# A post-norm stack of eight layers on one core: the last sequence's output map and norms in two halves of 128 tokens

## The chip, the core and the metric

The kernel runs on one core of one Trainium2 chip. A core has five engines that run side by side and wait for one another by semaphores: PE (matrix products and transposes), DVE (elementwise and reductions), ACT (functions and copies), POOL (elementwise) and SP (which issues most DMAs). The metric is the device time of one execution in microseconds; times are medians of several runs.

## The reference, cut to what matters

Eight layers in a row, each with a residual and a norm over the 128 features. Only the last two matter here: an attention over 8 sequences of 256 tokens with 16 heads of 8 features, and a linear map with ternary weights. The reference works them out like this (the four kinds of heads, rotation and decay, are left out):

```python
out = jnp.einsum('bhqk,bhkd->bhqd', attn, v)
out = jnp.transpose(out, (0, 2, 1, 3)).reshape(b, n, H * dh)
return out @ w_o
...
w_eff = w_ternary * alpha
out = jnp.einsum('bsd,od->bso', input, w_eff) + bias
...
x = _layernorm(x + _L3_attn_ref(x, ...), axis=-1)
x = _layernorm(x + _L3_ffn_ref(x, ...), axis=-1)
```

So after the attention every token goes, by itself, through the output map, a norm, the ternary map and a second norm. The attention is causal: the first 128 tokens of a sequence look at 128 keys, the last 128 at 256.

## The kernel before, in words

The program has six stages; the change is in the last, `typed` (from L2301), which computes the two layers above. Its work comes in 48 units, six for each of the 8 sequences. A unit is written (t, r0, r1): t = 0 takes the first 128 tokens, t = 1 the last 128, and r0 to r1 picks heads. So a sequence has the units (0, 0, 4), (0, 4, 8), (1, 0, 2), (1, 2, 4), (1, 4, 6), (1, 6, 8): two for the first half of its tokens and four for the second. The text names them by the first two numbers.

Each unit goes through the same steps, spread over four rounds of the loop over `i`: scores on PE (`sc`, with the decay and the mask added by small matmuls), row maxima on DVE (`nm`, L2254), Exp on ACT (`e`, L2259), the division by the sums on POOL (`e`, L2262), eight transposes on PE (`pt`, L981), two copies to SBUF on DVE or ACT (`ptsb`, L983), and 16 small matmuls into the output tile (`o`, called at L2271). The tile `o` holds one sequence, features by 256 tokens, in the one PSUM bank with the tag O: units with t = 0 fill its columns 0 to 127, the others columns 128 to 255.

After the sixth unit of a sequence comes its tail, the generator `after` (L2305): ACT copies `o` to SBUF (`ot`, L2308); PE multiplies by the output map (`wo`, four matmuls for the two token tiles); DVE adds the residual (L2316); `token_norm` (L942) takes statistics on DVE (L948, L949), Ln and Exp on ACT (L951, L952) and scales on DVE (L955); `channels` (L957) transposes the two tiles on PE (`zt`, L961) and copies them on ACT (`s_t`, L962), while POOL adds the bias rows (L2321); PE multiplies by the ternary map (`lin`); DVE adds (L2328); a second norm, a second pair of transposes and a last copy (`s3`) follow, and SP writes 128 x 256 values to the output (L2334).

Four results of a tail pass through PSUM: `wo`, `zt`, `lin` and `zt` again. All of them take the tag M, which has a single bank in this stage (`BANKS`: A=2, B=2, O=1, M=1). So do the projections of the next sequences.

A tail is not written in one piece. Its steps are put, as a generator, into the queue `side`, and the loop takes up to three steps per round from the head of that queue; a generator is finished before the next in the queue begins.

The order in which this writes instructions down is not the order in which the engines get them. At the end of the build the class `_Order` plans the whole program: it follows a model of the engines with a table of lengths, and at each moment gives a free engine the ready instruction with the lowest rank. A rank is the instruction's place in the program plus an offset from the table `BIAS`, by engine, tile name and stage (for instance 4960 for `DVE nm` in this stage, and 1645 for `DVE st`). The offsets and lengths were set for the program as it was; the change leaves them as they are. Two of the planner's rules matter here:

```python
if self.rings[tag][next_[tag]] != k:
    return None
...
if t.space == PSUM and self.ops[j][1] != e:
    self.edge(j, i)
```

The first: the tiles of one tag get their buffers strictly in program order. The second: two engines that use the same PSUM tile keep their program order, whichever columns they use.

Of the kernel before, what the change touches and what calls it, by code (L numbers as in the profile page):

```python
# [14 lines left out]
F32 = mybir.dt.float32  # L15
BF = mybir.dt.bfloat16
I32 = mybir.dt.int32
AF = mybir.ActivationFunctionType
ALU = mybir.AluOpType
# [4 lines left out]
P = 128  # L24
B = 8
S = 256
# [745 lines left out]
class _Kernel:  # L772
# [169 lines left out]
    def token_norm(self, src, dst, small, eps=EPS):  # L942

        nc = self.nc
        st = small.tile([P, 2, 6], F32, tag="st", name="st")
        mv = small.tile([P, 2, 2], F32, tag="mv", name="mv")
        for t in range(2):
            nc.vector.bn_stats(st[:, t, :], src[:, t, :])  # L948
            nc.vector.bn_aggr(mv[:, t, :], st[:, t, :])  # L949
        rs = small.tile([P, 2], F32, tag="rs", name="rs")  # L950
        nc.scalar.activation(rs, mv[:, :, 1], AF.Ln, bias=eps)  # L951
        self.norm = nc.scalar.activation(rs, rs, AF.Exp, scale=-0.5)  # L952
        yield
        for t in range(2):
            nc.vector.tensor_scalar(dst[:, t, :], src[:, t, :], mv[:, t, 0:1], rs[:, t : t + 1], ALU.subtract, ALU.mult)  # L955

    def channels(self, z, dst, copy, tag="M"):  # L957

        ps = self.psum(tag, "zt")
        for t in range(2):  # L960
            self.nc.tensor.transpose(ps[:, t * P : (t + 1) * P], z[:, t, :], self.ident)  # L961
        copy(dst, ps[:, 0:S])  # L962

    def softmax(self, small, work, sc, groups, keys, tag):

# [1335 lines left out]
    def typed(self):  # L2301
        nc, work, small = self.nc, self.ty, self.tys
        we, decay, inputs, before = self.we, self.decay, self.inputs, self.typed_before

        def after(b, o):  # L2305
            cs = bass.ts(b, S)
            ot = work.tile([P, S], F32, tag="ot", name="ot")
            nc.scalar.copy(ot, o)  # L2308
            yield
            ps = self.psum("M", "wo")[:, 0:S]  # L2310
            for t in range(2):
                ts = slice(t * P, (t + 1) * P)
                self.mm(ps[:, ts], ot[:, ts], self.w3[:, 640:768], t == 0, t == 1)
            s = work.tile([P, 2, P], F32, tag="s", name="s")
            flat = lambda a: a.rearrange("p t d -> p (t d)")
            nc.vector.tensor_add(flat(s), ps, flat(self.rows(b)))  # L2316
            yield from self.token_norm(s, s, small)
            yield
            st = work.tile([P, S], F32, tag="st", name="s_t")
            self.channels(s, st, nc.scalar.copy)  # L2320
            nc.gpsimd.tensor_tensor(s, s, self.bias3.unsqueeze(1).to_broadcast([P, 2, P]), ALU.add)  # L2321
            yield
            ps = self.psum("M", "lin")[:, 0:S]
            for t in range(2):
                ts = slice(t * P, (t + 1) * P)
                self.mm(ps[:, ts], st[:, ts], we, t == 0, t == 1)
            s2 = work.tile([P, 2, P], F32, tag="s2", name="s2")
            nc.vector.tensor_add(flat(s2), ps, flat(s))  # L2328
            yield from self.token_norm(s2, s2, small)
            yield  # L2330
            s3 = work.tile([P, S], F32, tag="s3", name="s3")
            self.channels(s2, s3, nc.scalar.copy)
            yield
            nc.sync.dma_start(self.out[:, cs], s3)  # L2334

        units = [(b, u) for b in range(B) for u in [(0, 0, 4), (0, 4, 8)] + [(1, r, r + 2) for r in range(0, 8, 2)]]
        n = len(units)
        side = deque([chain(self.results(1, work), before(1))])
        scs, es, o = {}, {}, None

        for i in range(n + 3):
            last = pts = None
            if i >= 3:
                pts = self.typed_transposed(es.pop(i - 3), work)
                last = self.last
            if i < n:
                b, u = units[i]
                while b not in inputs:  # L2350
                    if next(side[0], True):
                        side.popleft()
                scs[i], last = self.typed_scores(u, *inputs[b][:2], decay, last)
            if 0 <= i - 1 < n:
                es[i - 1] = self.typed_softmax(units[i - 1][1], scs.pop(i - 1), work, small)
            for _ in range(2):
                if side and next(side[0], True):
                    side.popleft()
            if i >= 3:
                b, u = units[i - 3]  # L2360
                if u[:2] == (0, 0):
                    o = self.psum("O", "o")[:, 0:S]
                    if b + 2 < B:
                        side.append(self.results(b + 2, work))
                self.typed_outputs(u, pts, inputs[b][2], o, last)
                if u[:2] == (1, 6):
                    rest = after(b, o)
                    next(rest)
                    if b + 2 < B:
                        side.append(before(b + 2))  # L2370
                    side.append(rest)
            if side and next(side[0], True):
                side.popleft()
        for g in side:
            for _ in g:
                pass
# [34 lines left out]
```

## Time and profile before

| what | value |
|---|---|
| median of three runs | 1642.47 us (1641.91 to 1643.14) |
| the profiled execution's own time | 1644.68 us |
| its span, first to last instruction | 1642.9 us |
| PE busy in the span | 1417.4 us (86%) |
| DVE, ACT, POOL busy | 1102.3, 968.6, 587.5 us |
| last sixteen matmuls of `o` end | 1629.43 us |
| last copy ends, output DMA is issued | 1638.31, 1638.34 us |
| mean granted clock of PE | 0.942 |

Positions are microseconds from the start of the span. In the timeline a line shows the start, the time taken, the engine, the line of the kernel, the operation and its tiles with their sizes; "x16" joins sixteen instructions in a row, and brackets tell how long the engine had been idle and what ended that. In the chain of waits a line is a piece of the chain that ended last: start, time, engine, tile and line; "issue" is a moment in which the engine waited for nothing that the profile shows. In the table by stretches a line gives from:to, length, then the busy time and number of instructions of PE, PE's weight loads, DVE, ACT and POOL, then the granted clock, the DMA share and GB/s.

### The profile page before, as it was taken

Reading aid. Unit: us, or ns where it says so; the run is one execution under the profiler, and the core shown is the slowest. Engines: PE = TensorE matmul, PEld = TensorE weight load, DVE = VectorE, ACT = ScalarE, POOL = GpSimd, SP = SyncE. Lnnn points to the kernel's source line nnn. Section 1 sums busy time; section 2 is a strip of 40 time slices with the busy share of each in tenths; the row PEclk is TensorE's granted clock in tenths of the full one; section 3 lists DMA queues with packets and bytes.
Section 4 is the critical chain, followed back from the end, with each engine's and each line's share of the span. In section 5 each row is a group of like instructions: output and inputs, shape, how many; then the busy total and the mean of one; then the engine's idle time right before and its main releaser. Section 6 shows DMA issues by size and latency. Waiting matters only on the chain. (4 is left out here: it accounts for less than half of the span.)

```text
span 1642.9 us, 28581 instructions
## 1 busy us (share of the span) xinstructions
PE 1417.4 (86%) x10826; PEld 909.4 (55%) x10826; DVE 1102.3 (67%) x2182; ACT 968.6 (59%) x2656; POOL 587.5 (36%) x535
## 2 busy tenths in 40 slices
PE   2688998989898887777579999999998899899997
PEld 1354554545554544334366766777675576556664
DVE  5745568898989898698545557554546333279886
ACT  3777888787978869446125545455453222167775
POOL 1334544535462523101431222212212102467774
PEclk7789999989999999779789999999998899999998
DMA  5000012121212223155430000000000130000000
GB/s 199 1 1 1 1 40 65 40 60 45 65 40 65 53 52 91 52 179 189 151 119 1 8 12 11 10 5 8 32 18 24 46 121 26 26 9 8 5 8 11
DMA packets 45113, 77.97 MB, mean 47 GB/s; under 512 B 5580, under 2 KB 21988, under 8 KB 43824
## 3 DMA queue, kind: packets, MB, share of 16 engines
q1 hardware_dynamic: 39648, 70.02, 14.0%
q0 software_dynamic: 3216, 5.07, 1.1%
q8 instruction: 85, 1.39, 0.4%
q10 hardware_dynamic: 2112, 1.05, 0.2%
q14 instruction: 52, 0.43, 0.1%
HBM read 66.87 MB, written 10.76 MB: 47 GB/s over the span
## 5 line engine op out<-in xcount | busy, mean ns | idle before, releaser
L870 PE MATMUL y<-hs,ident 128*128 128x512 f32 x256 | 139.7, 659 | 35.9 <-DVE hs L1307 35.6
L1158 POOL TENSOR_TENSOR e<-e,rc 128x1024 f32<-128x1024 f32 x32 | 78.0, 2437 | 202.7 <-DVE rc L1157 194.3
L1306 DVE TENSOR_TENSOR_SCAN hs<-da,hs 128x1024 f32<-128x1024 f32 x64 | 149.1, 2331 | 0.2
L2259 ACT ACTIVATE e<-sc,nm 128x128 f32<-128x128 f32 (+1 forms) x256 | 105.2, 427 | 46.6 <-DVE nm L2254 40.3
L1153 ACT ACTIVATE e<-sc,nm,rn 128x128 f32<-128x128 f32 x256 | 114.3, 466 | 13.8 <-DVE nm L1148 13.5
L981 PE MATMUL pt<-ident,e 128*128 128x128 f32 x768 | 114.2, 278 | 9.4 <-POOL e L1158 4.9
L1302 ACT ACTIVATE da<-d,na 128x255 f32<-128x255 f32 x256 | 109.3, 504 | 17.5 <-DVE hs L1306 13.7
L1836 POOL TENSOR_TENSOR e<-e,rc 128x512 f32<-128x512 f32 x32 | 34.0, 1064 | 219.8 <-DVE rc L1835 154.2
L981 PEld LDWEIGHTS pt<-ident,e 128*128 128x128 f32 x768 | 88.5, 141 | 42.5 <-issue 16.1
L2262 POOL TENSOR_TENSOR e<-e,rc 128x1024 f32<-128x1024 f32 x48 | 90.8, 1896 | 39.1 <-DVE rc L2261 32.1
L1105 POOL TENSOR_TENSOR t<-t,t 128x512 f32<-128x512 f32 x64 | 83.9, 1316 | 58.0 <-DVE t L1092 51.6
L1811 ACT COPY kp<-kps 128x512 f32<-128x512 f32 x128 | 74.7, 583 | 49.0 <-PE kps L870 46.4
L1658 POOL DMA_INDIRECT got<-ybuf,get x48 | 45.7, 952 | 159.2 <-DMA ybuf<-ys 97.1
L870 PEld LDWEIGHTS y<-hs,ident 128*128 128x128 f32 x256 | 48.5, 205 | 82.5 <-DVE hs L1307 54.2
L1304 DVE TENSOR_TENSOR hs<-u,bc 128x1024 f32<-128x1024 f32 x64 | 84.3, 1328 | 2.9 <-POOL u L1291 2.9
L1307 DVE TENSOR_TENSOR hs<-hs,bc 128x1024 f32<-128x1024 f32 x64 | 80.6, 1260 | 0.0
L1847 ACT COPY vs<-vps 128x512 f32<-128x512 f32 x64 | 37.4, 585 | 67.1 <-PE vps L870 53.6
L983 DVE COPY ptsb<-pt 128x512 f32<-128x512 f32 x104 | 68.8, 675 | 11.6 <-PE pt L981 9.3
L870 PE MATMUL qk<-w_local,h 128*128 128x512 f32 x128 | 69.3, 631 | 7.5 <-DVE t L1092 7.1
L870 PE MATMUL vps<-sa_vp,x_lf 128*32 128x512 f32 x512 | 68.4, 594 | 0.0
L1847 DVE COPY vs<-vps 128x512 f32<-128x512 f32 x64 | 43.3, 682 | 37.2 <-PE vps L870 25.1
L2057 DVE TENSOR_TENSOR sh<-sh,pu 128x512 f32<-128x512 f32 x32 | 22.0, 688 | 67.1 <-PE pu L870 54.0
(380 smaller groups left out, 3782.4 us busy)
## 6 DMA issues: line engine op xcount, KB each, us to landing
bc<-xs SPq DMA_DIRECT2D x128, 256.0 KB
w_moe<-in_e_dram SPq DMA_DIRECT2D x16, 768.0 KB
w_attn<-in_w_dram SPq DMA_DIRECT2D x4, 1024.0 KB
w_local<-in_w_dram SPq DMA_DIRECT2D x2, 1557.0 KB
places<-zeros SPq DMA_DIRECT2D x2, 1280.0 KB
got<-places SPq DMA_DIRECT2D x6, 256.0 KB
ybuf<-ys SPq DMA_DIRECT2D x8, 160.0 KB
x_in<-in_x_dram SPq DMA_DIRECT2D x1, 1024.0 KB
```

Source lines behind the costliest of these rows:

```text
L870: return self.nc.tensor.matmul(out, lhsT, rhs, start=start, stop=stop)
L981: self.last = self.nc.tensor.transpose(pt[:, j * P : (j + 1) * P], src[:, j * P : (j + 1) * P], self.ident)
L1105: nc.gpsimd.tensor_add(t1, t1, t2)
L1153: nc.scalar.activation(e[:, j, g, :], scs[:, j, g, :], AF.Exp, bias=nm[:, j, g : g + 1], scale=rq[:, j, g : g + 1], accum_out=sm[:, j, g : ...
L1158: nc.gpsimd.tensor_tensor(e, e, rc.unsqueeze(3).to_broadcast([P, 2, 4, P]), ALU.mult)
L1302: nc.scalar.activation(da[:, n, c, 1:S], d[:, c, 1:S], AF.Exp, scale=na[:, i : i + 1])
L1304: nc.vector.tensor_tensor(hs, u.unsqueeze(1).to_broadcast(shp), bn, ALU.mult)
L1306: nc.vector.tensor_tensor_scan(line(hs), line(da), line(hs), 0.0, ALU.mult, ALU.add)
L1307: nc.vector.tensor_tensor(hs, hs, cn, ALU.mult)
L1847: i = copy(v[:, c, :, :].rearrange("p a b -> p (a b)"), ps)
L2259: nc.scalar.activation(e[:, i, :], sc[:, i, :], AF.Exp, bias=nm[:, i : i + 1], accum_out=sm[:, i : i + 1])
L2262: nc.gpsimd.tensor_tensor(e, e, rc.unsqueeze(2).to_broadcast([P, n, keys]), ALU.mult)
```

## The change

For the last sequence (b = 7) the tail is run twice, each time for 128 tokens. The first half starts after the unit (0, 4), when columns 0 to 127 of `o` are complete: `after(b, o, (0,))` is begun there (its `ot` copy), and its other steps go to the end of the queue `side`. The second half starts after (1, 6), as the whole tail did. `after`, `token_norm` and `channels` take the number of token tiles from their operands. The other sequences' tails are as before.

In program order the last users of the bank M are now these (before, the last two groups were one with both token tiles):

```
sequence 6: wo, zt, lin, zt        between units (6: 1,6) and (7: 0,4)
first half of 7: wo, zt, lin, zt   between units (7: 0,4) and (7: 1,4)
second half of 7: wo, zt, lin, zt  after unit (7: 1,6)
```

For one half there are two matmuls in place of four in `wo` and `lin`, one transpose in place of two, adds and copies over 128 columns in place of 256, one `bn_stats`, one `bn_aggr` and one scaling in place of two, Ln and Exp over one column in place of two, and an output DMA of 64 KB in place of 128 KB.

```diff
--- before.py
+++ after.py
@@ -942,24 +942,26 @@
     def token_norm(self, src, dst, small, eps=EPS):
 
         nc = self.nc
+        n = src.shape[1]
         st = small.tile([P, 2, 6], F32, tag="st", name="st")
         mv = small.tile([P, 2, 2], F32, tag="mv", name="mv")
-        for t in range(2):
+        for t in range(n):
             nc.vector.bn_stats(st[:, t, :], src[:, t, :])
             nc.vector.bn_aggr(mv[:, t, :], st[:, t, :])
         rs = small.tile([P, 2], F32, tag="rs", name="rs")
-        nc.scalar.activation(rs, mv[:, :, 1], AF.Ln, bias=eps)
-        self.norm = nc.scalar.activation(rs, rs, AF.Exp, scale=-0.5)
+        nc.scalar.activation(rs[:, 0:n], mv[:, 0:n, 1], AF.Ln, bias=eps)
+        self.norm = nc.scalar.activation(rs[:, 0:n], rs[:, 0:n], AF.Exp, scale=-0.5)
         yield
-        for t in range(2):
+        for t in range(n):
             nc.vector.tensor_scalar(dst[:, t, :], src[:, t, :], mv[:, t, 0:1], rs[:, t : t + 1], ALU.subtract, ALU.mult)
 
     def channels(self, z, dst, copy, tag="M"):
 
+        n = z.shape[1]
         ps = self.psum(tag, "zt")
-        for t in range(2):
+        for t in range(n):
             self.nc.tensor.transpose(ps[:, t * P : (t + 1) * P], z[:, t, :], self.ident)
-        copy(dst, ps[:, 0:S])
+        copy(dst, ps[:, 0 : n * P])
 
     def softmax(self, small, work, sc, groups, keys, tag):
 
@@ -2302,36 +2304,37 @@
         nc, work, small = self.nc, self.ty, self.tys
         we, decay, inputs, before = self.we, self.decay, self.inputs, self.typed_before
 
-        def after(b, o):
-            cs = bass.ts(b, S)
-            ot = work.tile([P, S], F32, tag="ot", name="ot")
-            nc.scalar.copy(ot, o)
+        def after(b, o, ts=(0, 1)):
+            n = len(ts)
+            cols = slice(ts[0] * P, (ts[-1] + 1) * P)
+            ot = work.tile([P, S], F32, tag="ot", name="ot")[:, 0 : n * P]
+            nc.scalar.copy(ot, o[:, cols])
             yield
-            ps = self.psum("M", "wo")[:, 0:S]
-            for t in range(2):
-                ts = slice(t * P, (t + 1) * P)
-                self.mm(ps[:, ts], ot[:, ts], self.w3[:, 640:768], t == 0, t == 1)
-            s = work.tile([P, 2, P], F32, tag="s", name="s")
+            ps = self.psum("M", "wo")[:, 0 : n * P]
+            for t in range(n):
+                tt = slice(t * P, (t + 1) * P)
+                self.mm(ps[:, tt], ot[:, tt], self.w3[:, 640:768], t == 0, t == n - 1)
+            s = work.tile([P, 2, P], F32, tag="s", name="s")[:, 0:n]
             flat = lambda a: a.rearrange("p t d -> p (t d)")
-            nc.vector.tensor_add(flat(s), ps, flat(self.rows(b)))
+            nc.vector.tensor_add(flat(s), ps, flat(self.rows(b)[:, ts[0] : ts[-1] + 1]))
             yield from self.token_norm(s, s, small)
             yield
-            st = work.tile([P, S], F32, tag="st", name="s_t")
+            st = work.tile([P, S], F32, tag="st", name="s_t")[:, 0 : n * P]
             self.channels(s, st, nc.scalar.copy)
-            nc.gpsimd.tensor_tensor(s, s, self.bias3.unsqueeze(1).to_broadcast([P, 2, P]), ALU.add)
+            nc.gpsimd.tensor_tensor(s, s, self.bias3.unsqueeze(1).to_broadcast([P, n, P]), ALU.add)
             yield
-            ps = self.psum("M", "lin")[:, 0:S]
-            for t in range(2):
-                ts = slice(t * P, (t + 1) * P)
-                self.mm(ps[:, ts], st[:, ts], we, t == 0, t == 1)
-            s2 = work.tile([P, 2, P], F32, tag="s2", name="s2")
+            ps = self.psum("M", "lin")[:, 0 : n * P]
+            for t in range(n):
+                tt = slice(t * P, (t + 1) * P)
+                self.mm(ps[:, tt], st[:, tt], we, t == 0, t == n - 1)
+            s2 = work.tile([P, 2, P], F32, tag="s2", name="s2")[:, 0:n]
             nc.vector.tensor_add(flat(s2), ps, flat(s))
             yield from self.token_norm(s2, s2, small)
             yield
-            s3 = work.tile([P, S], F32, tag="s3", name="s3")
+            s3 = work.tile([P, S], F32, tag="s3", name="s3")[:, 0 : n * P]
             self.channels(s2, s3, nc.scalar.copy)
             yield
-            nc.sync.dma_start(self.out[:, cs], s3)
+            nc.sync.dma_start(self.out[:, b * S + cols.start : b * S + cols.stop], s3)
 
         units = [(b, u) for b in range(B) for u in [(0, 0, 4), (0, 4, 8)] + [(1, r, r + 2) for r in range(0, 8, 2)]]
         n = len(units)
@@ -2363,8 +2366,12 @@
                     if b + 2 < B:
                         side.append(self.results(b + 2, work))
                 self.typed_outputs(u, pts, inputs[b][2], o, last)
+                if b == B - 1 and u[:2] == (0, 4):
+                    rest = after(b, o, (0,))
+                    next(rest)
+                    side.append(rest)
                 if u[:2] == (1, 6):
-                    rest = after(b, o)
+                    rest = after(b, o, (1,)) if b == B - 1 else after(b, o)
                     next(rest)
                     if b + 2 < B:
                         side.append(before(b + 2))
```

## The prediction, made before the changed kernel was run

> **Names.** Six units make one sequence; the last sequence is number 7. R6 is the tail of output map, norms and second linear map of sequence 6; R7 the one tail of sequence 7 in the kernel before. A and B are its two halves after the change: A the first 128 tokens, B the last 128.
>
> **What bounds the kernel now.** I read the page first: a span of 1642.9 us, in which the change touches only the end. Then the chain of waits, from its last line backwards. From 1629.45 us on it has one strand, R7, with no other work on any engine; before that PE is nearly always busy (9.50 of 10 us in 1610 to 1620).
>
> ```profile
> 1628.77 0.66 PE o L870 x12
> 1629.43 0.02 issue
> 1629.45 0.38 ACT ot L2308
> 1629.83 0.04 issue
> 1629.88 0.73 PE wo L870 x4
> 1630.60 0.02 issue
> 1630.63 0.44 DVE s L2316
> ...
> 1633.74 1.24 PE lin L870 x4
> ...
> 1637.24 0.67 PE zt L961 x2
> 1637.91 0.02 issue
> 1637.94 0.37 ACT s L962
> ```
>
> The reader sees a dependent ladder: from ot (1629.45) to the end of the last copy (1638.31) it takes 8.86 us, and the output DMA is issued at 1638.34. So the end is set by when a tail's first step may start and by how long one ladder is. The start is the question. The timeline answers it with the sequence before:
>
> ```profile
> 1610.68 0.41 ACT L2308 COPY ot<-o 128x256 f32<-128x256 f32 x1
> ...
> 1614.05 0.39 ACT L962 COPY s<-zt 128x256 f32<-128x256 f32 x1
> ...
> 1614.66 0.61 PE L870 MATMUL wo<-w,ot 128*128 128x128 f32 x4
> ...
> 1617.13 0.65 PE L870 MATMUL o<-ptsb,vm 128*32 128x128 f32 x16
> ...
> 1627.32 0.37 ACT L962 COPY s<-zt 128x256 f32<-128x256 f32 x1 [1.51 <-PE zt L961]
> 1627.43 1.29 DVE L983 COPY ptsb<-pt 128x512 f32<-128x512 f32 x2 [0.63 <-PE pt L981]
> ```
>
> The ot of R6 is ready at 1611.09, but its wo starts only at 1614.66, after the last copy of the tail before it (1614.05 to 1614.44). That is the single M bank of this stage: wo, zt, lin, zt of all tails pass through it one after the other in program order, by the tile pool and by the planner's ring alike. R6 holds it from 1614.66 until its last copy ends at 1627.69: 13.03 us beside the units, against 8.43 us for R7 alone (1629.88 to 1638.31).
>
> **The change, part by part.** I follow the program order of the M bank: R6's wo, zt, lin, zt; then A's four; then B's four.
>
> 1. *The early ot of A.* The o of unit (0,4) ends at 1617.78 (last fence, 1617.13 + 0.65). ACT then has the two 0.20 us steps of R6's norm and idles until 1618.74, so the copy fits. It adds an order: the o of unit (1,0) writes the same PSUM tile and comes after ot. That o is at 1621.46, three microseconds later; behind it on PE stand lin of R6 and the next units, and their copies on DVE. Cost 0; without the cover at most the copy, 0.3. R6 gets no faster by it, since none of its instructions or waits changes.
>
> 2. *Where A starts.* A's wo could start at 1618, but the M bank is R6's until 1627.69. So wo of A starts at about 1627.76, in the gap of PE between the last transposes (1627.83) and the o of the last unit (1628.18). This is the step that takes the gain away: the half that was to run beside later units starts when one unit's o is left.
>
> 3. *Length of a half ladder.* I take R7's phases, start to start, and replace what gets shorter. No row shows these sums with 128 columns or two matmuls, so each is bounded by its neighbours. DVE add: 0.42 at 256 columns, 0.675 at 512, so 0.28 at 128 (between 0.17, a 128x6 op, and 0.42). ACT copy: 0.38 at 256, 0.585 at 512, so 0.28 (between 0.20 and 0.38). One bn_stats and one bn_aggr: 0.28 + 0.04 + 0.17 + 0.03 = 0.52 from the first to Ln, where two of each took 0.73. Ln and Exp stay 0.48; the scaling of one tile until zt starts stays 0.49 (0.36 and 0.14 in the chain). Fixed per norm: 0.32 + 0.52 + 0.48 + 0.49 = 1.81, two norms 3.62. Two copies with their hand-over 2 x 0.33 = 0.66. Together 4.28 us. The bias add of POOL (0.73 at 256; 0.53 by its slope to 1.90 at 1024) lies beside copy and lin and costs nothing; if it came last, 0.1.
>
> 4. *PE's part* depends on its clock:
>
> ```profile
> 1632.00:1633.00 1.00, 0.21 (x2) 0.19 (x2) 0.60 (x2) 0.23 (x2) 0.00 (x0) 1.00 0.00 0
> 1633.00:1634.00 1.00, 0.54 (x3) 0.35 (x3) 0.00 (x0) 0.37 (x1) 0.64 (x1) 0.77 0.00 0
> 1634.00:1635.00 1.00, 0.97 (x4) 0.67 (x4) 0.00 (x0) 0.00 (x0) 0.09 (x1) 0.50 0.00 0
> ```
>
> The first of the last three columns is the granted clock: 1.00 until 1633, then 0.50 to the end. Four matmuls of a product take 0.61 to 0.71 at full clock (wo) and 1.23 at half (lin); two transposes 0.44 and 0.66. So two matmuls with hand-over take 0.47 at full and 0.75 at half clock (bounds 0.3, one matmul, and 1.23), one transpose 0.33 and 0.43. A, mostly before 1633.5: 0.47 + 0.33 + 0.47 + 0.43 = 1.70, so 5.98 us. B, all at half clock: 0.75 + 0.43 + 0.75 + 0.43 = 2.36, so 6.64 us, of which 0.02 less at the end (no hand-over to PE): 6.62.
>
> 5. *A beside the last unit.* A's wo ends near 1628.2, but DVE copies ptsb until 1628.72 (second fence), so the add starts at 1628.76 where it could at 1628.23: +0.53. The ot of B needs ACT when the last o ends (1629.4), just beside A's Ln and Exp: +0.15. A ends 1627.76 + 5.98 + 0.53 + 0.15 = 1634.42.
>
> 6. *B.* Its ot is ready at 1629.8, and then waits some 4.6 us for the M bank. This is the new wait; behind it on PE stands only B itself. B runs from 1634.42 to 1641.04, where its DMA is issued; before it was 1638.34: +2.70.
>
> 7. *DMA.* 64 KB in place of 128 KB: the profile shows the transfer of 128 KB between 1639.1 and 1639.6, so half of 0.43 us goes: -0.2 (bounds 0 and -0.5). A's DMA lands long before. One more issue on SP (0.33 us) is beside B.
>
> Sum: +2.70 - 0.2 = +2.5 us. On the profiled execution (1644.68 us, span 1642.9) that is 1647.2; the three runs' median is 2.2 lower, and I add the difference to the median: 1642.47 + 2.5 = **1645.0 us**, +0.15%.
>
> **Rules weighed.** The Trainium skill, VectorE: DVE Perf Modes, section "The TRN2 errata", speaks against the change: a fixed latency is paid per instruction, so tiles should have 512 elements or more. The rows above carry the fixed part already; its formula, (N + 151) / 0.96 ns, would give an estimate of 0.29 in place of 0.28 for each of four adds, 0.04 more in all. The skill's TensorE: Matmul & The Clock Gate, Part 1, says that the clock halves after an idle window of about 3.4 us and stays up while PE counts as busy; if the thin work of A counted as busy, B would be at full clock.
>
> The bounds of the clock from the rows: B all at full clock takes 0.28 + 0.10 + 0.28 + 0.10 = 0.76 less (sum +1.7); A's lin at half clock too, 0.28 more, and no DMA gain, 0.2 more (+3.0).
>
> **Rivals.**
>
> *The early half is hidden.* A runs beside units (1,0) to (1,6) and is done by 1629.8. Then B alone follows its ot: wo at 1629.78, 4.28 + 0.47 + 0.33 + 0.75 + 0.43 = 6.26, DMA at 1636.0: -2.3 - 0.2 = -2.5, so 1640.0 us. For it: PE, DVE and ACT have room for some 6 us of A among the units. Against it: R6 in the bank until 1627.69, and 13 us was what R6 itself needed beside the units. 5 in 100.
>
> *A is late: the slower side.* Every delay of A's wo beyond 1628.3 passes on in full, since B waits for A. If the planner puts A's wo behind the last unit's o on PE (end 1629.43), it starts at 1629.45, and A's add at 1629.9 in place of 1628.76: +1.15, so +3.65 or 1646.1 us. From +3.28 on (0.2%, about what a measurement of this kernel can tell from no change) it counts as slower, that is when A's add comes 0.8 us later than 1628.76; the same holds if new ranks of later units make R6 leave the bank that much later. For it: the planner works with its own lengths, and more instructions shift the ranks of all that follow. Against it: in the trace the bank is free 0.4 us before the last o could start, and R6's ranks stand ahead of all that is shifted. 16 in 100.
>
> *It does nothing*: A and B overlap in part, since A leaves the bank between steps. The allocation order forbids it; something near 0 (+0 to +1), 5 in 100.
>
> *The forecast* (+1.7 to +3.2, so 1644.2 to 1645.7): 74 in 100.
>
> Low and high: 1643.3 leaves out the hidden half and most of the do-nothing case; 1646.6 takes in the late A (1646.1) with half a microsecond of scatter between runs (1641.91 to 1643.14 here). Faster by over 0.2% would need 1639.2, beyond even the hidden half: 3 in 100. Slower by over 0.2% is above 1645.75: the late A and the upper edge of the forecast, 22. Within 0.2%: 75.
>
> **What would show it.** Right: wo of A at 1627.7 to 1628.0, straight after R6's last copy; ot of B near 1629.8 and wo of B over 4 us later, after A's last copy; a half ladder of some 6 us in A and 6.6 in B; all up to 1627 unchanged. Wrong: a wo with two matmuls before 1627; B's wo straight behind its ot; R6's copies moved; or a different order of the units before 1617.

## The result and the profile after

The changed kernel took 1647.83 us (median of 7 runs, 1645.47 to 1650.27); the kernel before took 1641.91 us in the same comparison (7 runs, 1638.17 to 1646.88). The ratio is 1.0037, with a 95% interval of 1.0020 to 1.0054. A second measurement later gave 1.0017 (1.0001 to 1.0033). So the change makes the kernel slower, by 0.2 to 0.4%; the forecast of 1645.0 us had the sign, and was too small.

The traces are sharper than the times. On every engine the instructions stand in the same order in both kernels up to the start of the change (but for eight matmul records near 1120 us, whose order differs between two traces of the changed kernel as well), yet the start of `wo` of sequence 6's tail lies anywhere between 1611.70 and 1618.75 us in the nine executions profiled here: the scatter of the runs arises ahead of the change (near 64 us the traces of the two kernels and of the first four experiments are already 3.3 us apart). So everything below is counted from that `wo` ("from wo6"). From wo6 to the end of the span it is 28.23 us before (1614.66 to 1642.89) and 32.13 after (1613.88 to 1646.01): **+3.90 us**, which is 0.24%, and inside both intervals.

The timeline of the changed kernel (start, time taken, engine, line, tiles) shows the two halves:

```profile
1626.54 0.37 ACT L964 COPY s<-zt 128x256 f32<-128x256 f32 x1 [1.50 <-PE zt L963]
...
1626.96 0.49 PE L870 MATMUL wo<-w,ot 128*128 128x128 f32 x2
...
1628.67 0.27 ACT L2311 COPY ot<-o 128x128 f32<-128x128 f32 x1 [1.76 <-PE o L870]
...
1633.24 0.27 ACT L964 COPY s<-zt 128x128 f32<-128x128 f32 x1 [0.95 <-PE zt L963]
...
1633.56 0.80 PE L870 MATMUL wo<-w,ot 128*128 128x128 f32 x2 [0.35 <-ACT s L964]
...
1636.76 0.45 POOL L2324 TENSOR_TENSOR s<-s,bias 128x128 f32<-128x128 f32 x1 [6.19 <-PE zt L963]
...
1640.13 0.27 ACT L964 COPY s<-zt 128x128 f32<-128x128 f32 x1 [0.95 <-PE zt L963]
```

The issues of its output DMAs (count, then shortest/median/longest in ns, first and last start):

```profile
L2337 SPq DMA_DIRECT2D out_dram<-s x9: 332/333/358, 1491.9 to 1640.4; - x9
```

The first `wo` (A's) follows the last copy of sequence 6's tail by 0.05 us. B's `ot` is ready at 1628.93, but B's `wo` starts at 1633.56, 0.05 us after A's last copy. The output DMA is issued at 1640.42, 26.54 from wo6; before, it was 23.68. That is +2.86, and the end moved by 3.90: one microsecond is still missing. It is in what follows the last line of work. At the end of the program each engine's sequencer has an instruction `DRAIN`; in these traces the first one starts beside or behind the engine's last instruction, and the program does not end before all are done. In the same form, before:

```profile
L2407 POOLq DRAIN  x3: 46/97/8778, 1633.3 to 1642.6; - x3
L2407 SPq DRAIN  x3: 7/7/7, 1640.4 to 1642.4; - x3
```

and after:

```profile
L2414 POOLq DRAIN  x3: 46/97/8497, 1636.7 to 1645.7; - x3
L2414 SPq DRAIN  x3: 7/7/7, 1642.2 to 1645.5; - x3
```

POOL's last instruction is the bias add. After the change it is the one at 1636.76 in the timeline above; before, it stood here:

```profile
1633.36 0.72 POOL L2321 TENSOR_TENSOR s<-s,bias 128x256 f32<-128x256 f32 x1 [6.90 <-PE zt L961]
```

SP is through with the output DMA when its first drain starts: 1640.4 before, 1642.2 after. The end comes 2.5 and 3.8 us later, since another drain is still running: POOL's. It begins beside that add and lasts until 1642.10 (1633.33 + 8.78) and 1645.23 (1636.73 + 8.50). Counted from the end of that add (1634.09 and 1637.21) both are 8.02 us. The end of the span follows 0.78 us later in both. By this reading POOL's last instruction, not the output DMA, sets the end of both kernels, and that add came 3.90 us later (19.43 and 23.33 from wo6). The table of waits hides it: it puts SP's wait down to PE.

```profile
SPq L2414 <- PEq L2414: 3.6, 2, 3.2
SPq L2414 <- DMA out_dram<-s: 0.9, 1, 0.9
```

PE's own drain had ended by 1640.14; the releaser in such a line is the one that came last by its signal, and the chain that ends the program begins at POOL.

### The profile page after: what moved, and what is told of

It is laid out like the page before. It is cut to its first block, busy times and chain, and to the rows that moved or that the text cites. A ratio compares the mean times of both kernels' runs of the same rounds, so it can differ in the third digit from the quotient of the medians.

```text
span 1646.0 us, 28596 instructions
## 1 busy us (share of the span) xinstructions
PE 1419.0 (86%) x10826; PEld 909.1 (55%) x10826; DVE 1102.3 (67%) x2184; ACT 968.6 (59%) x2663; POOL 586.9 (36%) x536
## 5 line engine op out<-in xcount | busy, mean ns | idle before, releaser
L1304 ACT ACTIVATE da<-d,na 128x255 f32<-128x255 f32 x256 | 109.3, 503 | 17.3 <-DVE hs L1308 13.6
L2256 DVE TENSOR_REDUCE nm<-sc 128x4 f32<-128x1024 f32 (+1 forms) x48 | 58.1, 1211 | 12.5 <-PE sc L870 12.5
```

What stands on the lines that cost most here:

```text
L1304: nc.scalar.activation(da[:, n, c, 1:S], d[:, c, 1:S], AF.Exp, scale=na[:, i : i + 1])
```

## The experiments

Theory POOL says: the span ends 8.80 us (8.02 + 0.78) after POOL's last instruction, unless the output DMA lands later than that. Theory DMA says that the end follows the DMA. Theory BANK says that A was late, and B behind it, because of the single bank M; theory BUSY, that the engines had no room for A.

All runs in one table, in us from wo6; the last column is the ratio of times to the kernel before and its interval. The figures from wo6 come from one trace of each run; the two traces of the changed kernel (`after` and `after_again`) agree to 0.14 us.

| run | units' last `o` ends | output DMA issued | POOL's last ends | span ends | ratio |
|---|---|---|---|---|---|
| before | 14.75 | 23.68 | 19.43 | 28.23 | 1 |
| after | 14.74 | 26.54 | 23.33 | 32.13 | 1.0037 (1.0020 to 1.0054) |
| after_again | 14.75 | 26.39 | 23.19 | 31.99 | 1.0017 (1.0001 to 1.0033) |
| b_pool_late | 14.74 | 23.53 | 22.79 | 31.59 | 1.0023 (1.0008 to 1.0037) |
| b_bias_dve | 14.74 | 23.59 | 11.80 | 26.49 | 1.0000 (0.9986 to 1.0014) |
| a_bias_dve | 14.74 | 26.25 | 11.80 | 28.86 | 0.9997 (0.9985 to 1.0010) |
| a_own_bank | 16.33 | 23.10 | 19.90 | 28.69 | 0.9996 (0.9983 to 1.0010) |
| a_bank_dve | 16.33 | 23.03 | 13.65 | 25.64 | 0.9992 (0.9980 to 1.0004) |
| a_bank_late_rank | 15.58 | 22.54 | 14.49 | 25.17 | 0.9971 (0.9954 to 0.9989) |

**b_pool_late.** One more POOL instruction, at the very end of the last tail:

```diff
             self.channels(s2, s3, nc.scalar.copy)
+            if b == B - 1:
+                late = small.tile([P, 1], F32, tag="late", name="late", bufs=1)
+                nc.gpsimd.tensor_copy(late, s2[:, 1, 0:1])
```

> The kernel before with one more instruction: POOL copies one column (128x1) of s2 after the last norm of each sequence's... of the last sequence only, into a tile that nobody reads. Counted from the end of the last copy of the tail of sequence 6 (1627.69 us in the kernel before): the output DMA is issued 10.65 us later and the span ends 15.2 us later. Theory POOL (the end of the span is set by POOL: its last instruction, then about 8.02 us in which POOL drains, then 0.8 us): the last POOL instruction moves from 1634.08 to about 1637.3, so the span ends 18.4 us after that copy, 3.2 us later than before, while the output DMA is issued as early as before (10.6). Theory DMA (the end follows the output DMA): 15.2, no change. Time against the kernel before: 1.002 by POOL, 1.000 by DMA.

POOL in the timeline, and its drain:

```profile
1630.40 0.72 POOL L2321 TENSOR_TENSOR s<-s,bias 128x256 f32<-128x256 f32 x1 [6.90 <-PE zt L961]
1634.32 0.18 POOL L2335 COPY late<-s 128x1 f32<-128x1 f32 x1 [3.19 <-DVE s L955]
```

```profile
L2410 POOLq DRAIN  x3: 46/97/8222, 1634.3 to 1643.0; - x3
```

A copy of one column, which nobody waits for, ends at 1634.50; the drain lasts until 1642.51, 8.02 later, and the span ends at 1643.30. The DMA was issued no later than before (23.53). The end moved by +3.36 us from wo6 (18.6 us behind the last copy of sequence 6's tail, from which the expectation counts; 18.4 expected), and the time shows it: 1.0023, interval clear of 1. Theory DMA falls.

**b_bias_dve.** The kernel before, with the last sequence's bias add on DVE:

```diff
-            nc.gpsimd.tensor_tensor(s, s, self.bias3...to_broadcast([P, 2, P]), ALU.add)
+            (nc.vector if b == B - 1 else nc.gpsimd).tensor_tensor(s, s, self.bias3...to_broadcast([P, 2, P]), ALU.add)
```

> The kernel before, with the bias add of the last sequence's tail on DVE in place of POOL (128x256). Counted from the end of the last copy of sequence 6's tail. Theory POOL: POOL's last instruction is now the division of the last unit, which ends before that copy, so its 8.02 us are over by 7.5 us and the DMA's landing (1640.22 in the kernel before, 12.5 after the copy) sets the end: 13.6, that is 1.6 us earlier than before; the ladder up to the DMA's issue stays at 10.65, since DVE is idle while the last linear map runs. Theory DMA: 15.2, no change. Time against the kernel before: 0.999 by POOL, 1.000 by DMA.

```profile
1622.27 1.89 POOL L2262 TENSOR_TENSOR e<-e,rc 128x1024 f32<-128x1024 f32 x1 [0.53 <-DVE mv L949]
```

```profile
L2407 POOLq DRAIN  x3: 46/97/9937, 1622.2 to 1638.6; - x3
```

POOL's last instruction is now the last unit's division. The drain is done at 1632.18, again 8.02 us after that instruction, and no longer last. The DMA's issue stays (23.59), and the end comes 2.90 after it, 26.49 from wo6: 1.74 us earlier than before, 13.5 from the last copy of sequence 6's tail (13.6 expected). The ratio cannot tell 0.1% from nothing; its interval holds the 0.9989 that 1.74 us would be.

**a_bias_dve.** The changed kernel with the same edit, for both halves.

> The changed kernel, with the bias adds of both halves of the last sequence on DVE in place of POOL (128x128 each). Counted from the end of the last copy of sequence 6's tail (1626.91 us in the changed kernel, whose DMA is issued 13.51 later and whose span ends 19.1 later). Theory POOL: DMA's issue as before (13.5), the end about 16.1, 3.0 us earlier than the changed kernel, and 0.9 us later than the kernel before. Theory DMA: 19.1. Time against the kernel before: 1.0006 by POOL (1.0024 is the changed kernel by this count), 1.0024 by DMA.

The end is at 28.86 (15.8 from the last copy, 16.1 expected), 2.61 after the DMA's issue, 3.27 us earlier than in the changed kernel. With POOL out of the way the change costs 2.37 us (28.86 against 26.49): 2.66 later at the issue, and 0.29 given back by the smaller DMA. That is what the forecast had worked out (+2.70 and -0.2).

**a_own_bank.** The first half's four PSUM results take the tag A, whose two banks the scores use; the tag is handed on to `psum` and `channels` (cut to the lines for `wo`):

```diff
-        def after(b, o, ts=(0, 1)):
+        def after(b, o, ts=(0, 1), tag="M"):
...
-            ps = self.psum("M", "wo")[:, 0 : n * P]
+            ps = self.psum(tag, "wo", 1024 if tag == "A" else 512)[:, 0 : n * P]
...
-                    rest = after(b, o, (0,))
+                    rest = after(b, o, (0,), "A")
```

> The changed kernel, with the four PSUM results of the first half (wo, zt, lin, zt) in the banks with the tag A, which the scores use and which come free after the scores of the last units, in place of the single bank M. Theory BANK (the first half was late because the bank M was held by sequence 6's tail): wo of the first half starts some 6 us before the end of the last copy of sequence 6's tail, in place of right behind it, the first half runs beside the last units, and wo of the second half follows its ot within 0.1 us, about 2.1 us after that copy. The second half's ladder alone then gives the DMA's issue at about 8.4 us after the copy (13.5 in the changed kernel, 10.65 before). By theory POOL the end is then at 14.2 (POOL's last add at about 5.0 to 5.4, and 8.8): 1.0 us earlier than before, 4.9 earlier than the changed kernel; by theory DMA at about 11. Theory BUSY (the engines had no room for the first half before the last unit was done): wo of the first half still not before 1 us ahead of the copy, the end at 18 to 19. Time against the kernel before: 0.9994 by BANK and POOL, 1.002 by BUSY.

```profile
1622.01 0.25 ACT L2311 COPY ot<-o 128x128 f32<-128x128 f32 x1
...
1631.69 0.37 ACT L964 COPY s<-zt 128x256 f32<-128x256 f32 x1 [0.81 <-PE zt L963]
...
1635.13 0.27 ACT L2311 COPY ot<-o 128x128 f32<-128x128 f32 x1
```

```profile
1625.31 0.49 PE L870 MATMUL wo<-w,ot 128*128 128x128 f32 x2
...
1635.45 0.49 PE L870 MATMUL wo<-w,ot 128*128 128x128 f32 x2 [0.36 <-ACT ot L2311]
```

A's `wo` now starts 6.75 us before the last copy of sequence 6's tail ends (1632.06), and B's follows its `ot` by 0.05 us. Theory BUSY falls, BANK stands. But the expected end (14.2 from that copy) was missed, at 15.4: the units themselves finish 1.6 us later (16.33 in place of 14.75). The shared banks are not what holds them up, since the last unit's scores start where they did (4.07 from wo6 in both). In the trace A's `wo` and sequence 6's `lin` now stand ahead of two of a unit's transposes on PE, and A's add and sequence 6's add and statistics ahead of its copies `ptsb` on DVE (from 8.59, before from 7.48). The DMA is issued 3.44 us earlier than in the changed kernel, and the end, POOL's again, is at 28.69, which is +0.46 against before.

**a_bank_dve** has besides that the second half's bias add on DVE:

> The first half of the last sequence in the banks of the tag A, as in the run a_own_bank, and besides the bias add of the second half on DVE in place of POOL. Counted from the start of wo of sequence 6's tail, which comes before everything that is changed (1614.66 us in the kernel before, whose span ends 28.2 later; 32.1 in the changed kernel, 28.7 with the own bank alone). Theory BANK and POOL: the output DMA is issued at about 23.1 as with the own bank alone, and the end is no longer POOL's but the DMA's, 2.6 after its issue: 25.7. Theory DMA (the end follows the DMA by a fixed time, POOL plays no part): 28.7, as with the own bank alone. Time against the kernel before: 0.9985 by POOL, 1.0003 by DMA.

The DMA is issued at 23.03, the end is at 25.64, 2.61 after it (25.7 expected): the two causes add up, and together they turn the change into a gain of 2.59 us by the trace. The times do not tell that gain from none (0.9992, 0.9980 to 1.0004).

**a_bank_late_rank** also moves A's steps, after its `ot`, in the program behind the last unit, so that they rank below the units:

```diff
-                    side.append(rest)
+                    first = rest
                 if u[:2] == (1, 6):
...
+                    if b == B - 1:
+                        side.append(first)
                     side.append(rest)
```

> As a_bank_dve, but after its ot the steps of the first half stand in the program behind the last unit, so that the planner ranks them below the units' work (and still ahead of the second half). With the own bank alone the last matmul of the units ended 16.3 us after the start of wo of sequence 6's tail, 1.6 later than in the kernel before (14.75): the early half takes DVE and PE from the units. Theory RANK (that loss is due to the first half's rank): the last matmul of the units at 14.8 to 15.2, the DMA's issue at 21.7 to 22.1, the end at 24.3 to 24.7, some 3.7 us earlier than the kernel before. Rival (the first half now runs beside the second half's ladder and holds that up instead): the end at 25.5 or later. Time against the kernel before: 0.9977 by RANK, 0.9985 by the rival.

```profile
1619.98 0.49 PE L870 MATMUL wo<-w,ot 128*128 128x128 f32 x2
...
1622.72 0.41 PE L870 MATMUL o<-ptsb,vm 128*32 128x128 f32 x4 [0.97 <-DVE ptsb L985]
...
1628.38 0.63 PE L870 MATMUL o<-ptsb,vm 128*32 128x128 f32 x12
1629.38 0.49 PE L870 MATMUL wo<-w,ot 128*128 128x128 f32 x2 [0.36 <-ACT ot L2311]
```

The units' last `o` ends at 15.58, half of the loss won back: RANK expected 14.8 to 15.2. A's `wo` starts as early as with the high rank (6.55 from wo6 in both), and the order behind it is the same: sequence 6's add and statistics still go ahead of a unit's copies on DVE,

```profile
1621.06 0.42 DVE L2331 TENSOR_TENSOR s<-lin,s 128x256 f32<-128x256 f32 x1
1621.52 0.49 DVE L949 BATCH_NORM_STATS2 st<-s 128x6 f32<-128x128 f32 x2
1621.92 0.16 DVE L950 BATCH_NORM_AGGREGATE mv<-st 128x2 f32<-128x6 f32 x1
1622.01 0.66 DVE L985 COPY ptsb<-pt 128x512 f32<-128x512 f32 x1
```

and the unit's first `o` matmuls, which wait for that copy, come 9.29 from wo6, where they came 8.23 before. So the lower rank did not put these early steps behind the unit; why the planner orders them so is not shown. The end, 25.17, lies between RANK (24.3 to 24.7) and its rival (25.5 or later), so neither is fully right. It is the fastest version: 3.06 us earlier than before by the trace, 0.9971 by time (0.9954 to 0.9989).

**after_again.** The changed kernel once more:

> The changed kernel itself once more, for a narrower interval. By the ends counted from the start of wo of sequence 6's tail (32.1 against 28.2 us) the change costs 3.9 us, 1.0024, by POOL and BANK; if the first measurement's 1.0037 was more than scatter, something ahead of that wo is slower too, and the ratio stays at 1.003 to 1.005.

31.99 from wo6, and 1.0017: there is no sign that anything ahead of wo6 is slower, and the 1.0037 of the first measurement fits 0.24% and scatter.

## Why the prediction was wrong, step by step

- *The early ot* (1): as forecast. It took 0.25 us in ACT's idle time, and the order ahead of it is unchanged.
- *Where A starts* (2): right, 0.05 us after sequence 6's last copy, and for the reason given; a_own_bank shows the bank to be the cause. Step 5, A beside the last unit, was right in kind: A's add has to wait for DVE and starts 0.40 us after its `wo` ends (forecast: 1628.2 and 1628.76, so 0.56).
- *Half ladders* (3 to 6): A 6.60 us from `wo` to B's `wo` (6.66 forecast), B 6.86 (6.62). That A agrees is partly luck: its `lin` and its two transposes with their hand-over took 0.24 more than forecast (0.60, 0.36 and 0.51 for 0.47, 0.33 and 0.43), and the waits, norms and copies 0.3 less. B's part is 0.24 short: two matmuls with their hand-over took 0.84 and 0.90 at half clock, not 0.75, a lone transpose 0.51, not 0.43; the step from scaling to transpose gave 0.1 back each time. The DMA's issue moved by +2.86 where +2.70 was said.
- *The clock* (4): A's thin work did not keep it up. It fell 4.1 us after the units' last `o` in the changed kernel (from 1628.62; the granted share of 0.84 in 1632 to 1633, with 0.50 behind it, puts the fall at 1632.68) and 4.1 us after it in the kernel before. Over the nine traces this was 3.1 to 4.7 us, so 4.1 is not a fixed delay. So the branch of the Trainium skill's TensorE: Matmul & The Clock Gate, Part 1, in which A counts as busy was not taken.

```profile
1631.00:1632.00 1.00, 0.00 (x0) 0.00 (x0) 0.76 (x3) 0.14 (x1) 0.00 (x0) 1.00 0.00 0
1632.00:1633.00 1.00, 0.27 (x1) 0.18 (x1) 0.34 (x1) 0.26 (x2) 0.00 (x0) 0.84 0.00 0
1633.00:1634.00 1.00, 0.65 (x3) 0.44 (x2) 0.00 (x0) 0.27 (x1) 0.00 (x0) 0.50 0.00 0
```

- *The bias add of POOL "lies beside copy and lin and costs nothing"* (3), *and the end following the DMA* (7 and the sum): **this is the step that failed.** The forecast put the add at nothing. It was hidden for the ladder, but it was the last instruction of its engine, and 8.80 us after it the span ends. Before the change the DMA had 1.65 us of slack against that (23.68 + 2.90 = 26.58 against 28.23); after it 2.98. So neither the issue of the DMA nor its size counts, but how much later the last add comes: a whole half ladder and the first part of the next in place of the first part of one long ladder, +3.90 in place of +2.5. With POOL out of the way it is +2.37 (a_bias_dve against b_bias_dve). The profile of before had it: POOL's drain from 1633.3 for 8.78 us, and SP done at 1640.4 with an end at 1642.9. I read the chain of waits from its last line, and it ends at the last copy; the 4.6 us behind it I took for constant.
- *The rival on the slower side*: the time went there, but not by its mechanism. A was not late.
- *The range* (to 1646.6): what the end moved in the traces, 3.90, is 1.4 us more than the forecast's 2.5, and 1642.47 + 3.90 = 1646.4 is still inside. The first median, 1647.83, lies 1.5 us above that; the second of the same kernel is 1646.26. That part is scatter between runs.

What stays open: what POOL does in its 8.02 us, whether another kernel has them (this one also issues indirect DMAs from POOL earlier on, and no run is without them), and what exactly holds the units up by 0.83 us in the fastest version.

## What to carry to other kernels

Look for the end of the span behind the last line of the chain: list when each engine starts its last instruction and how long its drain runs, and treat the last instruction of an engine with a long drain as an end of its own. Before work is moved beside other work, follow every single-buffered resource that it passes through in program order; a generator may step early and its first tile still wait for the tail before it. And where runs scatter by more than the effect, count from an instruction ahead of the change: that resolved tenths of a microsecond here, where the medians could not resolve two.

## What the runs showed of the hardware that was not expected

The drain that POOL starts beside its last instruction ends 8.02 us (8.016 to 8.019 in nine profiled executions) after that instruction, whether this was a division over 1024 columns, an add over 256 or 128, or a copy of one column, and whether it ended 0.7 or 14.4 us before the last copy of the program did. Where this drain was the last to end (five of the nine), the span ends 0.78 us behind it. Not every drain of POOL is long: the one at the start of the program, beside some memsets, takes 0.19 us. With POOL out of the way the end came 2.90 us after the issue of a 128 KB output DMA, and 2.61 to 2.63 after one of 64 KB.
